# The experts' tiles: where a fetch stands in an iteration

## The chip, the cores and the metric

The kernel runs on one core of a Trainium2 chip. The core has five engines that run side by side, each through its own instructions in order: PE (matrix products and transposes), DVE (elementwise work and reductions), ACT (activations and copies), POOL (elementwise work and indirect transfers) and SP, which in this kernel reads registers from tables and issues DMA transfers. An instruction waits on semaphores; whatever stands behind a waiting instruction on the same engine waits as well. Sixteen DMA engines carry the transfers. The metric is the time of the program on the device in microseconds; the median of several runs is given.

## The reference

64 sequences of 128 rows of width 128 go through two layers of cross attention with a feed-forward part after each. The change lies in the first feed-forward part, a mixture of 8 experts of which each row takes two:

```python
for e in range(E):
    h1 = x_rep @ w1[e].T
    a, g = jnp.split(h1, 2, axis=-1)
    he = jax.nn.silu(a) * g @ w2[e].T
    out = out + jnp.where((expert_ids == e)[:, None], he, jnp.zeros((), out.dtype))
out = out * scores.reshape(-1, 1)
combined = out.reshape(N, TOP_K, h).sum(axis=1)
```

There are 8192 rows, hence 16384 pairs of a row and an expert. An expert's hidden width is 352 (padded to 384 in the kernel), everything in float32.

## The kernel before

The kernel goes through the first attention one sequence at a time. While it runs, a router chooses two experts for each row, and POOL scatters the normed rows, together with their shares, into a table in DRAM, `xs`, ordered by expert. Then comes the stage that matters here, `tile_stage`: 71 tiles of 256 rows, each of one expert. Their results go to a second table in DRAM, `ys`, from which POOL gathers each row's two results for the second attention. Two lists, a and b, tell a tile's expert and its first row in `xs`. List a holds the first 32 tiles (`NA`), which can start while POOL still scatters rows of later groups; list b holds the other 39. The second attention's first pieces of work are put between the last tiles.

For a tile t there are these parts:

- `fetch(t)` runs on SP alone. Two register loads (L881) read the tile's expert and row number from the list. Then three transfers are issued: the 256 rows from `xs` (L1079, 128 KB), the expert's weights (L1088, 576 KB), and the rows' shares (L1079 once more, 1 KB in 256 pieces of 4 bytes).
- `turn(t)`: PE transposes the rows (L1105), ACT copies them to `xT` (L1106).
- `hidden(t)`: six products with the first weights (L1115), ACT's silu (L1119) and DVE's multiplication (L1120), into a tile `p`.
- `project(t)`: six products with the second weights (L1128); DVE multiplies with the share and writes `y` (L1134); SP issues the store of `y` to `ys` (L1135).
- `between(t)`: other work of that iteration. In the early tiles it is the router's steps and scatters; each pair of scatters has a small POOL copy (`spacer`, L806) ahead of it that reads one element of the newest `y` (the probe), so that scatters don't run ahead. Later it is rows of zeros written behind each expert's rows (L1097), the making of list b and of the gather's addresses on DVE, and the first gathers (L1157) for the second attention.

Everything of a tile, rows, weights, `xT`, `y` and share, lies in one slot, a tile of the pools that the attention used. There are five slots (`SLOTS = 5`) in two kinds: t % 5 of 0, 1 and 2 take a buffer named `q4`, 3 and 4 one named `vc`. The profile shows them as q and vc. So tile t+3 is fetched into the slot of tile t-2, and the tile framework lets the first transfer into a slot wait until everything that used the old tile is done with it.

The order on every engine, SP's among them, is the program's order in this stage: the stage lies in a `manual_schedule` that names SP too. An iteration t has `turn(t+1)`, `hidden(t)`, `project(t-1)`, then `fetch(t+3)`, then `between(t)`. Iteration 0 has no project, and `between` starts with iteration 3. Tiles 0, 1 and 2 are fetched ahead of the loop. The first iterations stand between the last steps of the first attention. Ahead of the fetch of tile 32, the first of list b, a loop makes list b if it isn't made yet (`while "b" not in TILES`).

Of the kernel before, what the change touches and what calls it, by code (L numbers as in the profile page):

```python
# [44 lines left out]
def transformer_kernel(ctx, tc, a, out):  # L45
# [7 lines left out]
    for g in range(NG):  # L53
        t = resid.tile([S, GB, D], F32, name=f"x_{g}", tag=f"x_{g}")
# [825 lines left out]
    def value(ap, most):  # L880
        return nc.values_load(  # L881
            ap, engines=(ET.SP,), min_val=0, max_val=most,
            skip_runtime_bounds_check_because="it is clamped where it is made",
        )
# [165 lines left out]
    def tile_stage(work, mtile):  # L1050
# [6 lines left out]
        def slot(t):  # L1057

            if t % SLOTS < 3:
                s = work.tile([128, GB, NS, S], F32, name="q4", tag="q4", bufs=3)  # L1060
                return s.rearrange("p b s q -> p (b s q)")
            s = work.tile([128, GB, H // 2, 2, 32], F32, name="vc", tag="vc")
            return s.rearrange("p b h i w -> p (b h i w)")

        def fetch(t):
            te_i, tr_i = TILES["a" if t < NA else "b"]
            u = (slice(0, 1), slice(t, t + 1)) if t < NA else (slice(t - NA, t - NA + 1), slice(0, 1))
            e = value(te_i[u], E - 1)
            r = value(tr_i[u], E * CAP - TT)
            s = slot(t)  # L1070
            n = NF * 3 * 128
            w = s[:, :n].rearrange("p (c f) -> p c f", c=NF)
            x, y = (s[:, n + TT * k : n + TT * (k + 1)].rearrange("p (h d) -> p h d", h=2) for k in range(2))
            xT_of[t] = s[:, n + 2 * TT : n + 3 * TT]
            share = s[:, n + 3 * TT : n + 3 * TT + 2].rearrange("p (h d) -> p h d", h=2)
            first_ = scatters[: 2 * GA * GB]
            assert len(first_) == 2 * GA * GB
            for dst, src in ((x, xs[bass.ds(r, TT), :D]), (share, xs[bass.ds(r, TT), bass.ds(e + D, 1)])):
                f = nc.sync.dma_start(dst, src.rearrange("(h p) d -> p h d", p=S))  # L1079
                if t < NA:  # L1080

                    tc.declare_no_dep(
                        f.ins, group="scatters", keep=[s.ins for s in first_],
                        reason="rows of the first groups",
                    )
                    tc.add_to_no_dep_group("scatters", f.ins)
                if dst is x:
                    nc.sync.dma_start(  # L1088
                        w.rearrange("p c f -> p (c f)"),
                        a["w12"][bass.ds(e, 1)].rearrange("e p f -> p (e f)"),  # L1090
                    )
            w_of[t], x_of[t], share_of[t], y_of[t] = w, x, share, y
# [8 lines left out]
        def turn(t):  # L1101
            x = x_of.pop(t)
            pt = mtile()[:, :TT]
            for h in range(2):
                nc.tensor.transpose(pt[:, h * S : (h + 1) * S], x[:, h, :], ident)  # L1105
            nc.scalar.copy(xT_of[t], pt)  # L1106

        def hidden(t):
            w, xT = w_of[t], xT_of.pop(t)
            p = work.tile([128, 2, 4, 512], F32, name="p", tag="p").rearrange("p c a n -> p (c a n)")  # L1110
            hT = p[:, : NF * TT].rearrange("p (c t) -> p c t", c=NF)
            for c in range(NF):
                ph = mtile().rearrange("p (u t) -> p u t", u=2)
                for u in range(2):
                    nc.tensor.matmul(  # L1115
                        ph[:, u, :], lhsT=w[:, c, u * 128 : (u + 1) * 128], rhs=xT, start=True, stop=True
                    )
                sa = p[:, (NF + c) * TT : (NF + c + 1) * TT]
                nc.scalar.activation(sa, ph[:, 0, :], AF.Silu)  # L1119
                nc.vector.tensor_tensor(hT[:, c, :], sa, ph[:, 1, :], ALU.mult)  # L1120
            hT_of[t] = hT

        def project(t):
            w, hT = w_of.pop(t), hT_of.pop(t)
            po = mtile()[:, : 2 * D].rearrange("p (h d) -> p h d", h=2)
            for h in range(2):
                for c in range(NF):
                    nc.tensor.matmul(  # L1128
                        po[:, h, :], lhsT=hT[:, c, h * S : (h + 1) * S], rhs=w[:, c, 256:],
                        start=(c == 0), stop=(c == NF - 1),  # L1130
                    )
            y, share = y_of.pop(t), share_of.pop(t)
            for h in range(2):
                nc.vector.tensor_scalar(y[:, h, :], po[:, h, :], share[:, h, :], None, ALU.mult)  # L1134
            w = nc.sync.dma_start(ys[t * TT : (t + 1) * TT].rearrange("(h p) d -> p h d", p=S), y)  # L1135
            if "reads" in groups:
                tc.declare_no_dep(w.ins, group="reads", reason="other tiles")
            if t >= NA:
                tc.add_to_no_dep_group("writes", w.ins)
            written.append(w)  # L1140
            probes.append(y[0:1, 0, 0:1])
# [42 lines left out]
        def between(t):  # L1184

            rt = aside0.router
            if min(rt.due) < 1 << 30:
                for _ in range(2):
                    rt.call(probes[-1], mtile)
            elif zeros_left and "top" in TILES:  # L1190
                zeros(zeros_left.pop(0))
            for _ in range(2 if "b" in TILES else 1):
                next(aside0.steps, None)
            if t == NA + E:
                for _ in aside0.steps:
                    pass
            first_results(t)
            if t == NA:
                kvT = work.tile([D, GB, KF], F32, name="kvT", tag="kvT")
                kvT = kvT.rearrange("d b k -> d (b k)")[:, : GB * KC]  # L1200
                kvT = kvT.rearrange("d (b k) -> d b k", b=GB)
                nc.sync.dma_start(kvT, a["ctxT"][:, 0:GB, :])
                probes[0] = kvT
            if t == NA + 4:
                keys_of(l1, probes[0], 0, KC, mtile())
            if t == NA + 6:
                values_of(l1, probes[0], 0, KC, mtile())
# [7 lines left out]
        for t in range(NTL):  # L1215
            if t + 1 < NTL:
                turn(t + 1)
            hidden(t)
            if t:
                project(t - 1)  # L1220
            if t + 3 < NTL:
                if t + 3 == NA:
                    assert len(filled) == NG // 2 and not zeros_left
                    while "b" not in TILES:
                        next(aside0.steps)
                fetch(t + 3)
            if t > 2:
                between(t)
            yield
# [13 lines left out]
    class Aside0(Ahead):  # L1243
# [29 lines left out]
        def end(self, it, work, mtile):  # L1273

            for t in range(2 * (it - GB), 2 * (it - GB) + 2):

                if 0 <= t < NTL:
                    z = nc.sync.dma_start(
                        ys[t * TT : (t + 1) * TT].rearrange("(h p) d -> p h d", p=S), zero[:, :, :D]
                    )  # L1280

                    tc.add_manual_dep(z.ins, self.pace.ins.name, AFTER, reason="spread")
            if it == B - 2:
                self.tiles = tile_stage(work, mtile)
            if it >= B - 2:
                next(self.tiles)
# [279 lines left out]
```

## Time and profile before

| what | us |
|---|---|
| median of 3 runs | 1522.33 (1518.69 to 1523.64) |
| the profiled run's own time | 1516.1 |
| its span, first to last instruction | 1514.3 |
| PE busy | 1421.0 (94%) |
| DVE busy | 1102.4 (73%) |
| ACT busy | 847.6 (56%) |
| POOL busy | 640.4 (42%) |

The experts' products run from 619.6 us (the first product of L1115) to about 954 us. Busy times of three stretches of the stage, in us, with the granted clock of PE and DMA's share and rate:

| stretch | PE | DVE | ACT | POOL | clock | DMA share | GB/s |
|---|---|---|---|---|---|---|---|
| 615 to 655 | 35.11 | 17.72 | 18.23 | 24.82 | 0.96 | 0.48 | 137 |
| 655 to 708 | 45.68 | 29.89 | 20.32 | 31.59 | 1.00 | 0.70 | 205 |
| 708 to 945 | 225.95 | 122.07 | 81.24 | 30.29 | 1.00 | 0.69 | 201 |

In the first stretch the attention's last products mix with the first tiles; in the second POOL still scatters rows (its last scatter starts at 708.4); in the third the tiles are nearly alone.

In the profile's lines, DVE, ACT and POOL name engines, PEld is PE's loading of weights, and SPq stands for what SP's sequencer issues. In a group "out<-in" gives the program's names of what is written and read. An arrow from a waiting line to another line names who released the wait. A transfer's own piece in the chain of waits lasts from its issue to its landing.

### The profile page before, as it was taken

To read this page: it belongs to the slowest core of one execution; us is meant where nothing else is said; L and a number is where in the kernel's file an instruction comes from. 1 tells how busy PE (TensorE), PEld (TensorE's weight loads), DVE (VectorE), ACT (ScalarE), POOL (GpSimd) and SP (SyncE) were. 2 spreads that over 40 slices of the span, in tenths; PEclk is the share of its full clock that TensorE was granted. 3 is DMA by queue.
4 is the path that set the end of the run, shared out by engine and by line. 5 is a ranking of instruction groups with operands and counts; after the bars stand their busy time and mean duration, and the time that the engine had idled before them with its cause. 6 is when DMAs were issued, how large, how long until landed. Compare 5 with 4: busy or idle time off the path is not lost.

```text
span 1514.3 us, 42033 instructions
## 1 busy us (share of the span) xinstructions
PE 1421.0 (94%) x16620; PEld 1107.5 (73%) x16620; DVE 1102.4 (73%) x3024; ACT 847.6 (56%) x1740; POOL 640.4 (42%) x1195
## 2 busy tenths in 40 slices
PE   7999999999999999888999999898999999999987
PEld 5777777777777677777888888566666776767665
DVE  6777888888888988455754444687777778787763
ACT  4666666666666666543333333566667566666643
POOL 4123254646465635654001122377546555454210
PEclk9999999999999999999999999899999999999999
DMA  8433333333222221366766667111011111100000
GB/s 201 120 80 80 79 82 96 89 93 94 63 66 60 58 73 40 107 184 202 214 197 199 201 195 205 49 34 34 22 36 29 39 35 32 31 29 23 8 16 22
DMA packets 143719, 133.03 MB, mean 88 GB/s; under 512 B 48546, under 2 KB 126114, under 8 KB 141602
## 3 DMA queue, kind: packets, MB, share of 16 engines
q1 hardware_dynamic: 135330, 113.02, 27.3%
q0 software_dynamic: 8192, 17.32, 3.7%
q8 instruction: 132, 2.16, 0.6%
q14 instruction: 65, 0.53, 0.1%
HBM read 97.32 MB, written 32.97 MB: 86 GB/s over the span
## 4 chain that ended last, share of the span: by engine, by line
PE 69%; DVE 15%; DMA 4%; POOL 4%; ACT 4%; issue 2%; SPq 1%; POOLq 0%; DVEq 0%; ACTq 0%
PE bank L430 11%; PE bank L394 10%; PE bank L475 9%; PE bank L1115 9%; PE bank L1424 4%; PE bank L1445 4%; DVE nm L414 4%; PE bank L1128 3%; DMA q<-xs 2%; PE bank L407 2%; PE bank L214 2%; DVE q L462 2%; PE bank L511 2%; PE bank L681 2%; PE bank L202 2%
## 5 line engine op out<-in xcount | busy, mean ns | idle before, releaser
L414 DVE TENSOR_REDUCE nm<-bank 128x2 f32<-128x496 f32 (+1 forms) x768 | 463.5, 662 | 77.6 <-PE bank L430 61.8
L438 ACT ACTIVATE p<-bank 120x512 f32<-120x512 f32 (+1 forms) x768 | 402.1, 605 | 126.8 <-PE bank L430 123.9
L430 PE MATMUL bank<-q,k 32*120 32x256 f32 (+1 forms) x3072 | 438.1, 399 | 11.4 <-DVE nm L414 5.2
L430 PEld LDWEIGHTS bank<-q,k 32*120 32x120 f32 (+1 forms) x3072 | 293.5, 181 | 56.8 <-DVE nm L414 17.3
L394 PE MATMUL bank<-k,q 32*128 32x248 f32 x2048 | 291.0, 399 | 0.7 <-ACT q L334 0.5
L394 PEld LDWEIGHTS bank<-k,q 32*128 32x128 f32 x2048 | 202.2, 189 | 47.9 <-issue 11.0
L1120 DVE TENSOR_TENSOR p<-p,bank 128x256 f32<-128x256 f32 x213 | 88.0, 420 | 121.0 <-ACT p L1119 120.5
L475 PE MATMUL bank<-p,v 128*32 128x128 f32 (+1 forms) x4096 | 175.6, 275 | 0.2
L407 PE MATMUL bank<-k,qf 32*128 32x480 f32 x512 | 153.8, 602 | 0.8 <-ACT qf L295 0.8
L807 POOL DMA_INDIRECT xs<-xn,at x128 | 129.2, 1009 | 27.9 <-issue 24.3
L1119 ACT ACTIVATE p<-bank 128x256 f32<-128x256 f32 x213 | 81.0, 384 | 98.9 <-PE bank L1115 97.9
L484 ACT COPY ov<-bank 128x256 f32<-128x256 f32 x128 | 48.1, 376 | 143.5 <-PE bank L475 143.4
L475 PEld LDWEIGHTS bank<-p,v 128*32 128x32 f32 (+1 forms) x4096 | 108.8, 109 | 22.8 <-issue 13.7
L1364 POOL DMA_INDIRECT yb<-ys,back x112 | 108.5, 969 | 27.7 <-issue 19.5
L1115 PE MATMUL bank<-q 128*128 128x256 f32 x516 | 118.6, 379 | 1.6 <-ACT q L1106 1.6
L462 DVE SCALAR_TENSOR_TENSOR q<-bank,c_smask,q 128x256 f32<-128x256 f32 x256 | 111.1, 475 | 8.2 <-PE bank L459 7.8
L167 POOL TENSOR_SCALAR xn<-x,mv,rstd 128x128 f32<-128x128 f32 x252 | 110.2, 449 | 7.5 <-issue 1.4
L1115 PEld LDWEIGHTS bank<-q 128*128 128x128 f32 x516 | 94.7, 190 | 13.0 <-ACT q L1106 1.9
L475 PE MATMUL bank<-p,vc 120*32 120x128 f32 x2048 | 103.2, 272 | 0.0
L155 POOL TENSOR_SCALAR rstd<-mv 128x4 f32<-128x4 f32 x32 | 6.3, 198 | 219.9 <-DVE mv L113 123.0
L301 ACT ACTIVATE q<-bank,c_a_bq,c_hmask 128x512 f32<-128x512 f32 x124 | 90.1, 789 | 9.8 <-PE bank L292 9.8
L1157 POOL DMA_INDIRECT kvT<-ys,back x16 | 15.4, 961 | 189.7 <-DMA vc<-xs 114.0
(224 smaller groups left out, 2465.7 us busy)
## 6 DMA issues: line engine op xcount, KB each, us to landing
q<-in_w SPq DMA_DIRECT2D x43, 576.0 KB
vc<-in_w SPq DMA_DIRECT2D x28, 576.0 KB
vc<-in_ctx_v SPq DMA_DIRECT2D x16, 960.0 KB
ys<-zero SPq DMA_DIRECT2D x71, 128.0 KB
k<-in_ctx_k SPq DMA_DIRECT2D x32, 240.0 KB
q<-xs SPq DMA_DIRECT2D x43, 128.0 KB
ys<-q SPq DMA_DIRECT2D x43, 128.0 KB
x<-in_x SPq DMA_DIRECT2D x16, 256.0 KB
```

Source lines behind the costliest of these rows:

```text
L167: nc.gpsimd.tensor_scalar(xn[:, j, :D], xg[g][:, j, :], self.mv[:, b, 0:1], self.rstd[:, b : b + 1], ALU.add, ALU.mult,)
L301: nc.scalar.activation(q4s[g][:, :, s, :], pq.rearrange("p (b q) -> p b q", b=GB), AF.Identity, bias=w["bq"][:, s : s + 1], scale=hmask[:, ...
L394: nc.tensor.matmul(pa[:, u, :], lhsT=q4s[g][r, j, s, :], rhs=k2[g % 2][r, s // 2, j, :], start=True, stop=True,)
L407: lambda: nc.tensor.matmul(pa, lhsT=qfs[g][r, j, :], rhs=k4s[g][r, :, j, :], start=True, stop=True),
L414: nc.vector.tensor_reduce(nm[b % 2].rearrange("q i (a s) -> q a i s", s=16)[:, 2 * ra + v : 2 * ra + v + len(slots) // 2, :, 0], pa.rearra ...
L430: nc.tensor.matmul(pb[:n, v * 256 : (v + 1) * 256], lhsT=k2[g % 2][r, v, j, k0 : k0 + n], rhs=q4s[g][r, j, 2 * v : 2 * v + 2, :].rearrange ...
L438: nc.scalar.activation(ps_[b][:n, c, ra, :], pb[:n], AF.Exp, scale=SCALE)
L462: nc.vector.scalar_tensor_tensor(q, pm, smask[:, v : v + 1], q, ALU.mult, ALU.add)
L475: nc.tensor.matmul(pav[32 * ra : 32 * ra + 32, v * S : (v + 1) * S], lhsT=vs[g % 2][c][:, j, 4 * v + ra, i, :], rhs=p[:n, c, ra, (2 * v + ...
L807: s = nc.gpsimd.indirect_dma_start(xs, bass.IndirectOffsetOnAxis(at[:, j, k : k + 1], 0), xn, None)
L1115: nc.tensor.matmul(ph[:, u, :], lhsT=w[:, c, u * 128 : (u + 1) * 128], rhs=xT, start=True, stop=True)
L1364: nc.gpsimd.indirect_dma_start(y[:, k, b % 2, :], None, ys, bass.IndirectOffsetOnAxis(back[:, b, k : k + 1], 0),)
```

## The change

The fetch of tile t+3, with the loop that makes list b ahead of it, stands before `hidden(t)` and `project(t-1)` and no longer after them. `turn(t+1)` stays ahead of it and `between(t)` stays last. Nothing is added or removed.

```diff
         for t in range(NTL):
             if t + 1 < NTL:
                 turn(t + 1)
-            hidden(t)
-            if t:
-                project(t - 1)
+
             if t + 3 < NTL:
                 if t + 3 == NA:
                     assert len(filled) == NG // 2 and not zeros_left
                     while "b" not in TILES:
                         next(aside0.steps)
                 fetch(t + 3)
+            hidden(t)
+            if t:
+                project(t - 1)
             if t > 2:
                 between(t)
             yield
```

## The prediction

> **What bounds the stretch now.** I read the page's slices first, then the windows of the experts' stage, then the waits of PE and of SP, then the chain of waits, SP's timeline, and DMA traffic in half microseconds. The change touches only the stage from about 615 to 955 us. In the windows answer, the stretch from 708 to 945 us has PE busy for 225.95 of 237.00 us at a granted clock of 1.00, with a DMA share of 0.69 and 201 GB/s. PE is nearly the bound. What it still waits for there is almost one thing (waiter, releaser, us in total, times, longest):
>
> ```profile
> PE bank L1105 <- DMA q<-xs: 6.2, 16, 0.6
> PE bank L1105 <- DMA vc<-xs: 4.5, 11, 0.8
> ```
>
> The transposes of the next tile's rows (L1105) wait for these rows (q and vc are the two kinds of slot). The chain of waits (start, us, what) shows why:
>
> ```profile
> 879.20 0.34 ACT p L1119
> 879.53 2.14 DMA q<-xs
> 881.67 0.14 issue
> 881.80 0.41 PE bank L1105 x2
> 882.21 2.59 PE bank L1115 x12
> 884.80 1.34 PE bank L1128 x12
> 886.14 0.22 PE bank L1105 x2
> ```
>
> One PE iteration is 0.22 + 2.59 + 1.34 = 4.15 us, plus seams about 4.2. The rows were issued at 879.53, landed 2.14 us later, and PE stood. (The ACT piece is not what releases the issue: it starts before that activation ends.) SP's timeline shows what the issue stood behind:
>
> ```profile
> 877.89 0.37 SPq L1135 DMA_DIRECT2D ys<-q  x1
> 879.53 0.38 SPq L1079 DMA_DIRECT2D q<-xs  x1
> 880.10 0.35 SPq L1088 DMA_DIRECT2D q<-in_w  x1
> 880.70 0.37 SPq L1079 DMA_DIRECT2D q<-xs  x1
> 882.04 0.37 SPq L1135 DMA_DIRECT2D ys<-vc  x1
> 883.38 0.37 SPq L1079 DMA_DIRECT2D q<-xs  x1
> ```
>
> Each fetch (rows, weights, share) follows a store by 1.3 to 1.6 us: 0.37 to issue the store, then two register loads (L881, 0.28 and 0.27 to 0.57). The store waits for DVE's y, at the end of an iteration. So rows needed about 4.2 us after a store leave 1.5 us after it and land 3.7 us after it.
>
> Call X the time at which a fetch issues its rows. From tile 9 (X = 662.81) to tile 18 (708.29) X moves 45.5 us, 5.05 per tile. There the rows wait for POOL's copy of the probe (L806), which reads the slot that they overwrite:
>
> ```profile
> SPq L1079 <- POOL spacer L806: 8.1, 5, 2.2
> ```
>
> From tile 18 to tile 70 (941.89) it moves 233.6 us, 4.49 per tile.
>
> **The change, step by step.** No instruction is added or taken away; the fetch of tile t+3 (two register loads, three DMAs, their register work) moves ahead of hidden(t) and project(t-1). PE, ACT and POOL have nothing in the moved block, so their order stays. DVE's list loop moves too, but it has nothing left to do: list b's last conversion (L975) ran at 720.5, and its first register load at 770.6. On SP the order store(t-1), fetch(t+3) becomes fetch(t+3), store(t-1). Hence fetch(t+3) now follows directly on store(t-2).
>
> *What goes:* the wait of the rows behind store(t-1). This is worth at most PE's idle time there, 237.00 - 225.95 = 11 us.
>
> *What comes:* five slots turn round, so tile t+3 overwrites the slot of tile t-2, and y(t-2), which store(t-2) reads, lies in it. In the trace's records the rows issued at 879.53 check the semaphore of the store issued at 873.15, and those at 883.38 that of the store at 877.89: two stores back, landed long ago, so this wait costs nothing now. After the change that store is the instruction just ahead on SP. SP must stand from the store's issue to its landing, and queued behind stand weights, share and the next store, for which in turn the next fetch waits. This is a closed ring on SP and the DMA engines, with no PE in it: X, weights, share, store, store landed, next X. PE starves at its pace if it is over 4.2 us.
>
> *The ring's length.* Rows, weights and share take X + 1.17 + 0.37; the store follows at about X + 1.7. The trace marks a transfer sixteen times as its parts finish; I call it landed at the last mark. When does a store issued so soon land? Traffic by half microseconds for the fetch of 879.53 (columns: PE, PEld, DVE, ACT, POOL, clock, DMA share, GB/s):
>
> ```profile
> 879.50:880.00 0.50, 0.50 (x5) 0.45 (x4) 0.39 (x1) 0.08 (x1) 0.00 (x0) 1.00 0.02 2
> 880.00:880.50 0.50, 0.50 (x7) 0.50 (x6) 0.06 (x2) 0.38 (x1) 0.00 (x0) 1.00 0.07 9
> 880.50:881.00 0.50, 0.50 (x7) 0.50 (x6) 0.40 (x1) 0.00 (x0) 0.00 (x0) 1.00 0.73 174
> ...
> 883.50:884.00 0.50, 0.50 (x5) 0.42 (x4) 0.42 (x1) 0.02 (x1) 0.00 (x0) 1.00 0.51 141
> 884.00:884.50 0.50, 0.50 (x4) 0.45 (x3) 0.10 (x1) 0.36 (x1) 0.00 (x0) 1.00 0.09 17
> ```
>
> A microsecond of nothing, then 3.5 us in which rows, weights and the following store pass, then nothing again. The store of 882.04 left 2.5 us after X, had half its marks at X + 4.5 and its last at X + 5.5; the weights' last came at X + 4.4. The nearest rows to the new order are stores that already left soon after a fetch, in the scatter stretch: the one at 664.53, 1.72 us after X = 662.81, landed at X + 5.58, and five such (issued 1.7 to 2.2 after X) at 5.23 to 6.42, mean 5.66. From 760 us on, 17 stores issued 2.5 to 2.7 after X landed at 4.66 to 6.21, mean 5.25. Leaving earlier doesn't help: the store's marks come behind those of the weights. From the semaphore checked to the next rows issued the records show 0.18 us; I take 0.2.
>
> So the ring is 5.66 + 0.2 = 5.86 us while POOL scatters, and 5.25 + 0.2 = 5.45 after. The bounds: from below 4.66 + 0.2 = 4.86 (the best of the 17), from above 5.86 everywhere (stores of 708 to 760 averaged 6.05, but with transfers of zeros ahead of them, which fall behind the store in the new order). The register loads lie inside the wait.
>
> *A rule against this.* The Trainium skill, DMA: Bandwidth & Descriptors, section Anatomy of one DMA, fits one transfer (issued from GpSimd) as 2.0 us plus its bytes over 436 GB/s. For rows, weights, share and store together, 853 KB, that gives an estimate of 2.0 + 1.96 = 3.96, a ring of 4.2: no longer than PE's iteration, and the change would bring its 11 us. The rows above show about 250 GB/s in the busy part and last marks 0.7 us behind the middle ones. I take the rows.
>
> **The sum.** Tile 9's rows wait for POOL's copy, which ends at 662.79, whatever SP does; what the earlier fetches gain before is lost there. From then: 9 x 5.86 = 52.7 instead of 45.5 (+7.3), and 52 x 5.45 = 283.4 instead of 233.6 (+49.8): +57 us. From the last X to the end of the stage the work is PE's and the same; the second attention needs the stage's end, so nothing later takes it back. The span goes from 1514.3 to 1571; the profiled run was 1516.1, 1.8 more, so 1573. The median shown is 1522.33, above its profiled run; I carry the +57 over: 1579.
>
> **Rivals.**
> - *The ring is lighter* (0.17): late marks are chance of the old timing, and a ring of 4.86 later and 5.43 (5.23 + 0.2) in the scatter stretch gives 9 x 5.43 + 52 x 4.86 = 301.6 against 279.1: +22, 1545. For it: the middle marks at X + 4.5. Against: every late mark now counts, as the wait is for all sixteen.
> - *The ring is heavier* (0.15): 5.86 throughout, 61 x 5.86 = 357.5, +78: 1601. For it: the 6.05 of 708 to 760. Against: the quieter 5.25 after.
> - *PE stays the bound, faster* (0.05): if the store didn't queue behind the weights. A store with nothing ahead (868.93) landed in 1.82; 1.7 + 1.82 + 0.2 = 3.7 is under 4.2, the rows come early and 11 us go: 1511. It decides wherever the ring is under 4.2. Against it stand the stores at 664.53 and its like.
> - *No change* (0.03): a ring near 4.5, or an SP order that doesn't alter because something else releases the rows: 1522. Against: in this stage SP's order is the program's.
>
> My own case (ring 5.3 to 5.7, 1567 to 1593) has 0.60. The range 1546 to 1602 takes in both slower rivals' sums but for their outer halves, and leaves out the two others. A difference of 0.3% (4.6 us) is what can be told from none: faster 0.05, within 0.03, slower 0.92.
>
> **What would show it.** In the changed profile: rows (L1079) waiting on SP for the store's landing ("DMA ys"), some 2 us per tile, over 100 us in all; waits of SP's stores for DVE gone (they are 1 to 2 us a tile now); L1105 waiting for rows about 1.2 us per tile, some 70 us against 17.5; X at even steps of 5.4 us instead of 3.9 and 5.0 by turns; DMA traffic in the stage down from 201 to about 165 GB/s; PE's busy time unchanged. It is wrong if rows don't wait for the store, or if a store issued 1.7 us after X lands before X + 4.3.

## The result, and the profile after

| | before | after |
|---|---|---|
| median, us | 1520.51 (4 runs) | 1579.76 (4 runs, 1574.88 to 1583.17) |
| span of the profiled run, us | 1514.3 | 1573.0 |
| rows of tile 9 issued | 662.8 | 663.4 |
| tile 9 to 18, us per tile | 5.05 | 5.56 |
| tile 18 to 70, us per tile | 4.49 | 5.49 |
| from the rows of tile 70 to the end of the span | 572.4 | 574.3 |

The ratio of after to before is 1.0382 (95% interval 1.0359 to 1.0404): the changed kernel is 3.8% slower. The last four lines of the table come from the times at which SP issues a tile's rows. Their differences, 0.6 + 4.6 + 51.7 + 1.9 us, are together the 58.7 us between the two spans, but for rounding.

The waits of SP of the changed kernel, from 715 to 1005 us, about tile 18 to the end of the stage (waiter, releaser, us in total, times, longest):

```profile
SPq L1079 <- DMA ys<-q: 62.0, 31, 3.1
SPq L1079 <- DMA ys<-vc: 44.5, 21, 3.5
SPq L1135 <- DVE q L1134: 3.5, 9, 0.5
...
SPq L1135 <- DVE vc L1134: 1.8, 5, 0.5
```

The rows (L1079) now wait for the landing of the store, 52 times in 52 tiles, 2.05 us each. The wait of the stores for DVE, which stood in this place (29.3 and 19.5 us before in the like stretch), is down to 3.5 and 1.8 us. Here it is SP that comes late: in each of the 52 turns the result lay ready at least 3.1 us before its store left (5.2 us on average), while SP stood before the fetch. The waits of PE in the same stretch:

```profile
PE bank L1105 <- DMA q<-xs: 34.3, 30, 2.3
PE bank L1105 <- DMA vc<-xs: 19.0, 18, 2.5
```

The transposes waited 10.7 us in 27 waits before, and wait 53.3 us in 48 now. SP's timeline of the changed kernel shows one turn of the ring (start, us, engine, line):

```profile
905.65 0.37 SPq L1079 DMA_DIRECT2D vc<-xs  x1
906.22 0.35 SPq L1088 DMA_DIRECT2D vc<-in_w  x1
906.82 0.37 SPq L1079 DMA_DIRECT2D vc<-xs  x1
907.24 0.46 SPq L1135 DMA_DIRECT2D ys<-vc  x1
910.90 0.37 SPq L1079 DMA_DIRECT2D vc<-xs  x1
```

The store leaves 1.59 us after the rows, right behind the share. Then SP issues nothing for 3.2 us. By the trace's completion marks this store landed at 910.70, 0.2 us before the next rows left. In the chain of waits the transfers are pieces now, where ahead of the change nearly everything was PE:

```profile
912.49 3.34 DMA ys<-q
...
916.03 2.19 DMA q<-xs
918.22 0.14 issue
918.35 0.41 PE bank L1105 x2
918.76 2.59 PE bank L1115 x12
```

A store's landing releases a fetch (912.49 to 915.83), and the fetch's landing releases PE. What the DMA engines do meanwhile stands in the windows of half a microsecond around the issue at 910.90 (PE, PEld, DVE, ACT, POOL, clock, DMA share, GB/s):

```profile
909.50:910.00 0.50, 0.50 (x4) 0.45 (x3) 0.00 (x0) 0.30 (x1) 0.50 (x1) 1.00 0.40 111
910.00:910.50 0.50, 0.50 (x4) 0.45 (x3) 0.38 (x1) 0.09 (x1) 0.34 (x2) 1.00 0.13 39
910.50:911.00 0.50, 0.50 (x4) 0.44 (x3) 0.06 (x2) 0.39 (x1) 0.48 (x2) 1.00 0.00 0
911.00:911.50 0.50, 0.50 (x5) 0.46 (x4) 0.40 (x1) 0.07 (x1) 0.50 (x2) 1.00 0.00 0
```

The engines run dry: the end of one turn's traffic is waited for, and about 1.0 us passes after the issue before the first bytes of the next turn (by the packets' records, in most of the 52 turns). Over the whole stretch this reads as

```profile
715.00:1005.00 290.00, 235.19 (x1398) 209.21 (x1397) 123.97 (x342) 82.47 (x215) 30.15 (x40) 0.99 0.59 165
```

165 GB/s where it was 201, for the same bytes.

### The profile page after: what moved, and what is told of

The parts are those of the page before. It is cut to its first block, busy times and chain, and to the rows that moved or that the text cites. A ratio compares the mean times of both kernels' runs of the same rounds, so it can differ in the third digit from the quotient of the medians.

```text
span 1573.0 us, 42032 instructions
## 1 busy us (share of the span) xinstructions
PE 1432.9 (91%) x16620; PEld 1113.4 (71%) x16620; DVE 1103.0 (70%) x3024; ACT 847.8 (54%) x1740; POOL 642.6 (41%) x1195
## 4 chain that ended last, share of the span: by engine, by line
PE 63%; DVE 15%; DMA 11%; ACT 4%; issue 2%; POOL 2%; SPq 2%; POOLq 0%; ACTq 0%; DVEq 0%
PE bank L430 11%; PE bank L394 9%; PE bank L475 9%; PE bank L1115 6%; DMA ys<-q 5%; PE bank L1425 4%; PE bank L1446 4%; DVE nm L414 3%; DMA ys<-vc 3%; PE bank L407 2%; PE bank L1128 2%; PE bank L214 2%; DVE q L462 2%; DMA q<-xs 2%; PE bank L511 2%
## 5 line engine op out<-in xcount | busy, mean ns | idle before, releaser
L1115 PE MATMUL bank<-q 128*128 128x256 f32 x516 | 123.5, 391 | 1.6 <-ACT q L1106 1.6
L1115 PEld LDWEIGHTS bank<-q 128*128 128x128 f32 x516 | 98.2, 197 | 14.4 <-ACT q L1106 1.9
```

The source lines that it names most:

```text
L1115: nc.tensor.matmul(ph[:, u, :], lhsT=w[:, c, u * 128 : (u + 1) * 128], rhs=xT, start=True, stop=True)
```

## The experiments

Kernels of one batch ran on one chip, with the kernel of before beside them. On the chips of the first and third batches the kernel of before itself took 1575 us, on the others 1519, so ratios are compared, and times only within a batch. The columns below are us per tile between the issues of the rows.

| kernel | batch | time, us | ratio to before (95%) | tile 9 to 18 | tile 18 to 70 |
|---|---|---|---|---|---|
| y apart, whole fetch moved | 1 | 1546.27 | 0.9809 (0.978 to 0.9838) | 6.07 | 4.16 |
| y apart, order of before | 1 | 1570.88 | 0.9964 (0.995 to 0.9977) | 5.83 | 4.59 |
| rows alone moved | 1 | 1553.34 | 0.9859 (0.9833 to 0.9886) | 5.48 | 4.19 |
| store issued from ACT | 1 | 1560.56 | 0.9899 (0.9873 to 0.9926) | 5.50 | 4.31 |
| changed kernel again | 2 | 1574.76 | 1.0376 (1.0346 to 1.0406) | 5.83 | 5.48 |
| two thirds of the weights | 2 | 1537.47 | 1.0130 (1.0102 to 1.0158) | 5.26 | 4.76 |
| y apart, rows alone | 2 | 1491.54 | 0.9813 (0.9789 to 0.9837) | 4.41 | 4.23 |
| y apart, whole fetch again | 3 | 1546.75 | 0.9825 (0.9803 to 0.9846) | 6.07 | 4.17 |
| y apart, order of before again | 3 | 1570.61 | 0.9981 (0.9968 to 0.9995) | 5.82 | 4.58 |
| rows alone again | 3 | 1553.53 | 0.9858 (0.9841 to 0.9875) | 5.24 | 4.24 |
| y apart, whole fetch | 4 | 1491.41 | 0.9806 (0.9779 to 0.9832) | 4.44 | 4.18 |
| y apart, rows alone again | 4 | 1490.70 | 0.9823 (0.9798 to 0.9848) | 4.41 | 4.19 |

My theory was the closed ring: it needs the slot that is only free at the store's landing, and the store queued behind the weights. The rivals were that the transfers simply get into each other's way in the new order, that any wait for the store just ahead costs the time, and that the ring is fixed latency with no bytes in it.

**y apart, whole fetch moved.** The changed order, with y out of the slot; nothing else of the transfers' order or size is different.

```diff
-            y, share = y_of.pop(t), share_of.pop(t)
+            share = share_of.pop(t)
+            if t % 3 == 2:
+                y = work.tile([128, 2 * D], F32, name="yt", tag="yt", bufs=1)
+            else:
+                y = rows.tile([128, NV * S], F32, name="ov", tag="ov")
+            y = y.rearrange("p (h d) -> p h d", h=2)
```

> The changed order, but y of a tile lies in buffers of its own (three, taken in turn from two that the attention's output used and one new), no longer in the slot. So a slot is free once DVE has read the share, and the rows needn't wait for the store's landing; all transfers keep their order and size. Theory (closed ring over the store's landing): the ring is gone, PE is the bound again at about 4.2 us per tile, from tile 18 to tile 70 some 222 us instead of 285; time 1509, ratio to before about 0.993. Rival (the transfers get into each other's way, whatever waits for what): the order of the transfers is the changed one, so the time stays near 1579, ratio 1.035 or more.

Measured: ratio 0.9809, 4.16 us per tile. With the same transfers in the same order the loss is not only gone but turned into a gain. The rival of colliding transfers falls. The gain is larger than I had expected (0.993); what of it is explained is told further down. The chain of waits of this kernel on the chip of the fourth batch shows what bounds now:

```profile
860.92 0.22 PE bank L1105 x2
861.14 2.59 PE bank L1115 x12
863.73 1.34 PE bank L1128 x12
865.07 0.22 PE bank L1105 x2
865.28 2.59 PE bank L1115 x12
```

It is PE alone, one iteration in 4.15 us, with no wait. Its windows say the same of the stretch from 702 to 920 us:

```profile
702.00:920.00 218.00, 218.00 (x1367) 201.34 (x1366) 120.34 (x338) 80.71 (x211) 33.30 (x45) 1.00 0.79 219
```

The DMA engines carry 219 GB/s here, more than before the change (201), and neither PE nor SP shows a wait for a transfer in this stretch.

**y apart, order of before.** The same edit on the kernel before.

> The order of before with y in the same three buffers of its own. Theory: in the old order the rows wait for a store that landed long ago, so this alone changes nothing after tile 18 (4.49 us per tile, the rows still behind store(t-1)); only the scatter stretch may move, since POOL's copies now hold y's buffer and not the slot: 0 to 6 us less; time 1515 to 1521. Rival (keeping y in the slot costs something by itself): clearly faster than before, by 10 us or more.

Measured 0.9964 and, in the third batch, 0.9981; from tile 18 on 4.59 and 4.58 us per tile. So y's own buffers alone bring 0.2 to 0.4%, and most of what the first experiment gained came from the moved fetch. The move was worth something all along; in the changed kernel the ring hid it.

**Rows alone moved.** y stays in the slot; weights and share stay where they were.

```diff
+                rest = []
+                fetch(t + 3, rest)
             hidden(t)
             if t:
                 project(t - 1)
+            if t + 3 < NTL:
+                rest[0]()
```

(`rest` takes the issue of weights and share; the fetch with register loads and rows comes ahead of it.)

> Of the fetch only the two register loads and the rows' transfer stand before hidden(t); weights and share are issued after project(t-1) and its store. y stays in the slot. Theory: the rows still wait for the landing of the store just ahead, but that store no longer stands behind the weights, neither on SP nor on the DMA engines, and lands 1.8 to 2.2 us after its issue; the ring is then under 4.2 us and PE bounds: 4.2 to 4.3 us per tile from 18 to 70, SP's rows wait some 0.5 to 1 us per tile for the store, time 1509, ratio 0.993. Rival (any wait of the rows for the store just ahead is what costs): still slower than before, between 1530 and 1560.

Measured 0.9859 and 0.9858, 4.19 and 4.24 us per tile. SP's timeline in the first batch's run shows the order: store, weights (L1089 in this kernel), share, then the next tile's rows and the next store (L1143):

```profile
852.99 0.37 SPq L1143 DMA_DIRECT2D ys<-vc  x1
853.55 0.34 SPq L1089 DMA_DIRECT2D q<-in_w  x1
854.15 0.37 SPq L1079 DMA_DIRECT2D q<-xs  x1
855.98 0.37 SPq L1079 DMA_DIRECT2D vc<-xs  x1
857.14 0.37 SPq L1143 DMA_DIRECT2D ys<-vc  x1
```

The rows still check the landing of the last store before them. But the store leaves ahead of the weights, and while it lands SP issues weights and share. The waits of SP in that run, from 728 to 944 us:

```profile
SPq L1079 <- DMA ys<-q: 2.1, 4, 0.8
...
SPq L1079 <- DMA ys<-vc: 1.2, 3, 0.5
```

That is 3.3 us in 7 waits, against 106.5 us in 52 in the changed kernel, and less than the 0.5 to 1 us per tile that I had expected. A store lands 2.35 us after its issue here, and 3.65 in the changed kernel, where it stands behind 576 KB of weights. Since the wait itself is nearly gone, this kernel alone doesn't refute the rival that any such wait costs its time; the next one does.

**Store issued from ACT.** The changed order, `nc.scalar.dma_start` for the store.

```diff
-            w = nc.sync.dma_start(ys[t * TT : (t + 1) * TT].rearrange("(h p) d -> p h d", p=S), y)
+            w = nc.scalar.dma_start(ys[t * TT : (t + 1) * TT].rearrange("(h p) d -> p h d", p=S), y)
```

> The changed order, but the store of y is issued from ACT's queue and not from SP's; y stays in the slot, so the rows wait for the landing of store(t-2) as in the changed kernel. Theory (it takes both: the landing waited for, and the store behind the fetch on SP): the store leaves as soon as y is there, the ring is open, the rows wait some 2 us per tile on SP but early enough; PE bounds, about 1509, or up to 1520 if ACT, waiting for y ahead of the store, holds up its copy of the next rows. Rival (the landing wait alone makes it slow, wherever the store is issued): 1570 or more.

Measured 0.9899, 4.31 us per tile. The waits of SP from 728 to 944 us:

```profile
SPq L1079 <- DMA ys<-q: 38.1, 14, 3.9
SPq L1079 <- DMA ys<-vc: 25.0, 11, 3.8
```

The rows wait for the store's landing as long at a time as in the changed kernel, up to 3.9 us, but in only 25 of the stretch's 50 tiles. The store no longer waits its turn behind SP's fetch: from 851.56 to 872.30 the stores leave in even steps of 4.15 us, the pace of PE, while the steps of the rows are 2.5 us and up to 5.9 us by turns. So a late landing holds up one fetch and not the store after it, and the delays don't add up. PE waited for rows only twice in that stretch:

```profile
PE bank L1105 <- DMA q<-xs: 1.3, 2, 0.9
```

The rival that any wait for the store costs its time falls here. It takes both halves of the ring: the landing waited for, and the store behind the fetch. Of the 0.12 to 0.15 us per tile that this kernel is behind the first one (4.16) and the one with the rows alone moved (4.19), I can't say whether it is ACT's or the transfers'.

**The changed kernel again, and with two thirds of the weights.** In the second kernel a tile's fetch carries 384 KB of weights, and the products use the blocks that are there, so its result is another.

```diff
-                        w.rearrange("p c f -> p (c f)"),
-                        a["w12"][bass.ds(e, 1)].rearrange("e p f -> p (e f)"),
+                        w.rearrange("p c f -> p (c f)")[:, :768],
+                        a["w12"][bass.ds(e, 1)].rearrange("e p f -> p (e f)")[:, :768],
```

> The changed kernel itself once more, so that the other kernels of this chip have it beside them: the ring of 5.3 to 5.6 us per tile from tile 18 to tile 70, ratio to before 1.033 to 1.042 if the ring is a matter of transfers and not of one chip.

> The changed kernel, but each tile fetches 384 KB of weights and not 576 KB; the products take the blocks that are there (block k modulo 6), in the same number and shapes, so the output is another one. Theory (the ring is one latency plus the time of the bytes that stand ahead of the store, about 250 GB/s in the busy part): 192 KB less make the ring 0.77 us shorter, 4.7 instead of 5.5 us per tile from 18 to 70, 40 us less there and some 4 in the scatter stretch: ratio to before about 1.010, between 1.003 and 1.018. Rival (the ring is latency of the waits on SP alone): unchanged, 1.035 or more. Rival (PE bounds as soon as the ring gives a little): below 1.

Measured: the changed kernel again has 5.48 us per tile from 18 to 70, the same as on the first chip. With 192 KB less the ring is 4.76, shorter by 0.71 us, and the ratio 1.013. That is about 275 GB/s for the bytes taken away, near the 250 read off the busy windows. The store's landing comes 2.93 us after its issue, where it was 3.65: the 0.71 us are the store's. Fixed latency on SP is excluded as the whole of the ring, and PE isn't the bound at once: the rows still wait for the store, as its waits of SP from 720 to 930 us show:

```profile
SPq L1079 <- DMA ys<-q: 34.1, 26, 1.9
SPq L1079 <- DMA ys<-vc: 29.7, 18, 3.0
```

**The two edits together, and which of them is best.**

> y in buffers of its own and, of the fetch, only register loads and rows ahead of hidden(t); weights and share after project(t-1). Theory: with y apart PE had no wait left from tile 18 on (4.16 us per tile), so putting weights and share back can't help there; 4.15 to 4.2 us per tile, ratio 0.979 to 0.985, as with y apart and the whole fetch moved. Rival (weights and share far ahead still cost the store or the rows something): faster than that by 5 us or more, ratio 0.977 or less.

> y apart with the whole fetch moved, beside y apart with the rows alone moved, on one chip: is one of them better? With PE the bound from tile 18 on in both (4.16 to 4.23 us per tile), only the stretch before can differ. Theory: no difference that can be told, ratio to before 0.979 to 0.985. Rival (weights fetched far ahead crowd the rows and the scatters in the early tiles): this one is slower by 5 us or more, its time from tile 0 to tile 18 longer by as much.

> y apart with the rows alone moved, beside the kernel ahead of this on one chip. Theory: as that one, ratio 0.979 to 0.985. Rival (weights far ahead crowd the early tiles): faster than that one by 5 us or more, with 4.4 to 4.8 us per tile from 9 to 18 where that one has more than 5.

With y apart it makes no difference whether weights and share move with the rows: 0.9806 and 0.9823 on one chip, with overlapping intervals, 4.44 and 4.41 us per tile in the scatter stretch. Both beat the kernel before by 1.8 to 1.9% and the changed one by over 5%.

**The scatter stretch, not settled.** With y apart, tile 9 to 18 took 4.4 us per tile on the chips of the second and fourth batches; the kernel before had 5.05 on the first chip, whose times agree with theirs. The third batch was to tell whether y's leaving the slot or the order did this.

> y apart in the changed order once more, beside the two next ones on one chip, to split the gain between the scatter stretch (tile 9 to 18) and the rest. From 18 to 70 PE bounds at 4.16 to 4.23 us per tile against 4.49 to 4.59. If it is y's leaving the slot that shortens the scatter stretch (POOL's copy holds y's buffer and no longer the slot), this kernel and the next show 4.4 to 4.8 us per tile there against 5.05 or more; if it is the order, this and the third do. Ratio to before 0.979 to 0.985.

> y apart in the order of before once more. From 18 to 70 as before, 4.45 to 4.6 us per tile; scatter stretch as said for the kernel ahead of this: 4.4 to 4.8 if y's leaving the slot shortens it, 5 or more if the order does. Ratio 0.994 to 0.999.

> Rows alone moved, y in the slot, once more. From 18 to 70 4.18 to 4.25 us per tile; scatter stretch 4.4 to 4.8 if the order shortens it, 5 or more if only y's leaving the slot does. Ratio 0.983 to 0.989.

On that chip none came near 4.4: 6.07, 5.82 and 5.24 in this order. There this stretch is set by other things too (in the first of the three PE waits 5.3 us in one place for the router's DVE work), and no kernel with only one of the two edits ran on a chip where the effect shows. With y apart the waits of the rows for POOL's copy are gone from SP's waits, which fits y's leaving the slot, but this is argued and not shown. What stays open is not small: of the 23.7 us by which the span of y apart with the whole fetch moved (fourth batch, 1490.6) is shorter than that of before, 16.3 lie from tile 18 to 70 and 8.8 ahead of tile 18, 3.3 of these ahead of tile 9; behind tile 70 it is 1.4 longer.

## Why the prediction was right

- **What bounds.** PE with waits for rows: right, but what goes was mis-sized. I put it at PE's idle time, at most 11 us. On the chip of the fourth batch tile 18 to 70 took 217.36 us instead of 233.61, so it was 16.3. PE's busy time hides a part of a wait, as PE's timeline before the change shows at a seam without a wait and at one with it:

```profile
885.31 0.83 PE L1128 MATMUL bank<-vc,p 128*128 128x128 f32 x6
885.98 0.38 PE L1105 MATMUL bank<-ident,q 128*128 128x128 f32 x2
...
890.78 0.41 PE L1105 MATMUL bank<-ident,vc 128*128 128x128 f32 x2 [0.49 <-DMA vc<-xs]
```

Without a wait the transposes begin 0.16 us before the products ahead of them have ended (886.14), and add 0.22 us to PE's busy time; after a wait nothing lies beside them, and they add 0.41. 27 waits of 0.19 are 5 us, and 11 + 5 are the 16. The prediction's own figures held this: 52 tiles at 4.2 us are 218.4, 15 less than 233.6.

- **The ring.** Step by step as foreseen: the rows check the store just ahead, the store leaves 1.64 us after X on average (foreseen 1.7), its last mark comes behind that of the weights, 3.65 us after its issue, and 0.19 later the rows leave. That is 5.48 of the 5.49 us measured, where 5.45 was put. That leaving earlier doesn't help came true as well: these stores left nearly 1 us sooner after X than the 17 of before, and landed at X + 5.30 where those had 5.25.
- **The scatter stretch.** 5.56 us per tile, where 5.86 was put; the repeat on another chip had 5.83. So 4.6 us were lost there and not 7.3: this term was too large.
- **Tile 9 and the tail.** Tile 9's rows left 0.6 us later, as POOL's copy for which they wait ended at 663.34 and not at 662.79, and 1.9 us came behind tile 70; both were put at nothing. Together with the 1.9 us by which the ring was too short they make up for the scatter stretch: 57 foreseen, 58.7 measured in the spans. That the sum came out so close is in part luck.
- **The rule of the skill.** The Trainium skill's fit for one transfer (DMA: Bandwidth & Descriptors, section Anatomy of one DMA), 2.0 us plus bytes over 436 GB/s, gave an estimate of 4.2 us for the ring when put to the four transfers together. Measured is 5.49, and the stores of before had told it better. In the experiment with fewer weights the bytes taken away had moved at about 275 GB/s.
- **The rivals.** A lighter ring (4.86) and a heavier one (5.86 throughout) are both out by the 5.49 (the lighter one's sum, 1545, lies 1 us below the range that I gave). That PE stays the bound is what the open rings do, but the changed kernel isn't one. Its time was put at 1511, and with y apart as well the open rings give 1491: 16.3 us and not 11 from tile 18 on, and the 8.8 ahead of it, which the prediction has at nothing.
- **The signs.** Waits of the rows on SP of some 2 us per tile (2.05), the traffic at 165 GB/s, stores that no longer wait for DVE: as said. PE's waits for rows over the stage were put at some 70 us and are 62.0. The steps of X were to be even at 5.4; they run from 5.0 to 6.7, by the late marks. PE's busy time was to stay and rose from 1421.0 to 1432.9: the longer transposes and the clock (below), whose parts weren't told apart.

## What to carry to other kernels

Before a load is moved ahead of a store, ask what the load's buffer is waiting for: where the buffer holds the store's source, the load waits for the landing of the store that now stands just ahead of it, and if the store in turn queues behind the load's bytes, the two form a ring with a pace of its own, here 5.49 us against PE's 4.15. Keep the results that a store reads out of the buffer that the next load fills (three buffers of 1 KB per partition did it here), or move only the small transfer that is late, or issue the store from another engine. A wait can cost PE more than its idle time shows: without it, the first products would have begun before the last ones had ended (0.19 us per wait here).

## What the runs showed of the hardware beyond that

- A 128 KB store landed 1.82 us after its issue with nothing ahead of it, and 3.65 us (mean of 52) behind 705 KB, though the sequencer had issued all of that in 1.6 us. The last of the sixteen marks decides: in the changed kernel it came 0.2 to 2.0 us after the middle one, and the rows left 0.2 us behind it.
- A starving PE also loses clock. The granted clock was 1.00 before from 655 us on, and in the changed kernel 0.94 from 655 to 715 and 0.99 after; four times between 655 and 1005 us its records fall to one half for 3.4 us. In the 3.4 us ahead of each of the four PE was busy for 0.9 to 1.1 us. The Trainium skill, TensorE: Matmul & The Clock Gate, section Part 1: The HAM clock gate, has the clock halved after an idle window of about 3.4 us; the length agrees, but PE was not wholly idle in these. It cost nothing here: from tile 9 on every result lay ready at least 3.1 us before its store left, in these turns too.
- Two groups of chips gave the same kernel of before 1519 and 1575 us. The ratios of the same two kernels, run on both, agree within their intervals (whole fetch with y apart: 0.9809, 0.9825 and 0.9806), and so does what bounds from tile 18 on; the early tiles do not. The granted clock of the kernel before differs too, 0.97 on average on the slower chips and 0.99 on the others, but that is less than the 3.7% between the times. What sets the groups apart stays open.
